# Two product-quantised layers of a vision block: where the tables' last rows are loaded and subtracted

## The chip, the cores and the metric

The kernel runs on one core of a Trainium2 chip. The core has five engines that run side by side, each with its own queue of instructions: TensorE (PE in the profile; its weight loads are PEld), VectorE (DVE), ScalarE (ACT), GpSimd (POOL) and SyncE (SP), which here only issues DMA transfers. The metric is the device time of one execution in microseconds (us); lower is better. Before the change three runs gave 3858.85 (median), 3858.28 and 3866.12.

## What is computed

The whole is a convolution block of three product-quantised layers (1024 to 256 channels, 3x3 on 256, 256 to 1024), and then an attention layer that the change does not touch. The first part, cut to what matters:

```python
def _amm(patches, centroids, lut, inv_temp):
    v = patches.reshape(B, ncb, sub, H * W).transpose(0, 3, 1, 2)
    scores = 2.0 * jnp.einsum('blcs,cks->blck', v, centroids) \
        - jnp.sum(centroids * centroids, -1)[None, None]
    attn = jax.nn.softmax(scores * inv_temp, axis=-1)      # over K = 16
    out = jnp.einsum('blck,cko->blo', attn, lut)

out = _amm(_gn(x), c1_centroids, c1_lut, c1_invt)          # layer 1
out = relu(_bn(out, bn1_g, bn1_b))
out = _amm(_extract3x3(out, 1), c2_centroids, c2_lut, c2_invt)  # layer 2
out = relu(_bn(out, bn2_g, bn2_b))
...
```

x is 32 images of 1024 x 14 x 14. A codebook has 16 entries, and its softmax weights over the 16 sum to one. So the sixteenth weight is one less the other fifteen: the table's sixteenth ("last") row can be subtracted from the other fifteen rows and need not have a weight of its own. This is what "last rows" means below.

## The kernel before

`layers()` builds the three layers in order; each engine runs its instructions in the order in which they are written, and waits by semaphores for what other engines and transfers must have finished. SP is one such queue: a transfer that must wait holds all transfers behind it. POOL's and DVE's orders are fixed in the same way.

**Units.** Layers 1 and 2 run 128 units each: 16 pairs of images times 8 groups b of codebooks. For one unit, `units()` writes score matmuls (PE), the exponential into a tile t (ACT, L595), a transpose (DVE, L607), in layer 1 a halving add (POOL, L610), the sum over 16 (DVE, L625), the reciprocal (L627), its transpose r (DVE, L633), the product t*r (POOL, L637), and then the table matmuls of PE (`lut`, L698): 16 of them, or 12 for b = 0 and 4. The scores run 4 units ahead of the table matmuls in layer 1, 3 in layer 2 (`ahead`), and t rotates over `ahead + 2` tiles. The order is written out by hand in the loop of `units()`: the scores of unit i + ahead, the softmax of an earlier one, its transfers, then `side(i)` (whatever else is due), then the table matmuls of unit i.

**Spare places.** 15 of 16 rows of t hold weights; the places of the sixteenth are used for more codebooks. Every fourth unit (b = 0 or 4) makes a "spare" block (L635), and `spare_rows` (L680) copies its rows into the free places of that unit's and the next three units' t, by 3 or 4 small transfers on SP. The table matmuls wait for these.

**Tables.** Each layer has 8 tables (`packed_lut`), in 8 weight tiles that layers 1 and 2 share: `own` loads the table's rows (L424), `others` the rows for the spare places (L427). `last_rows(d, layer, b)` loads the last rows, broadcast, to a place d: 3 or 4 transfers of 128 KB (L439) and, in its own `others`, one for the spare places (L442); `less` then subtracts d from the table (L445), on POOL. The table matmuls of unit b cannot start before that.

In layer 1, the first loads are x of pairs 0 and 1, tables 0 and 1 with their last rows, tables 2 to 7, and then one unit at a time the last rows of 2 to 7, in places of the unused output tile; the subtraction of b is at i = b - 3. In layer 2, the tables come in during layer 1's last units, as each weight tile comes free (`luts2`), and the last rows go through two places "drop" in turn: `without_last(b)`, at i = b - 2, subtracts the last rows of b and loads those of b + 2.

**Between the layers.** After layer 1's last table matmuls come the batch norm's constants (DVE, and one power on POOL, L242), its application into the pads (ACT, L917), their store to DRAM (`store_pair`, "h1d", L928), and from there the loads of 3x3 patches (`load_patches`, L948) that layer 2's score matmuls (L1001) read; L1010 adds the ninth tap. Meanwhile `score_biases` (L375 a copy on POOL, L377 and on for DVE, the matmul L390) and `score_matrices` (L351) make layer 2's score weights from its centroids, and `wm` (L982) those of the ninth tap. `warm` is a row of matmuls without a use of their result.

Of the kernel before, what the change touches and what calls it, by code (L numbers as in the profile page):

```python
# [10 lines left out]
F32 = mybir.dt.float32  # L11
AF = mybir.ActivationFunctionType
ALU = mybir.AluOpType
# [4 lines left out]
P = 128  # L18
C = 1024
CT = C // P  # L20
HW = 196
N2 = 2 * HW
NC = 448
NCP = 416
TP = 105
KC = 16
W = 256
IMG = 225
# [5 lines left out]
def bc(ap, axis, n):  # L34

    u = ap.unsqueeze(axis)
    shape = list(u.shape)
    shape[axis] = n
    return u.to_broadcast(shape)
# [111 lines left out]
def conv_preact_kernel(ctx: ExitStack, tc: tile.TileContext, a: dict, out: bass.AP):  # L151
    nc = tc.nc
    x = a["x"]
    B = x.shape[0]
    NP = B // 2
# [62 lines left out]
    def kmasks():  # L218
        nc.vector.tensor_reduce(kmask, ident.rearrange("p (c k) -> p k c", k=KC), AX.X, ALU.add)
# [24 lines left out]
    def load_x(pool, p):  # L244
        xt = pool.tile([P, CT, N2], F32, tag="x", name=f"x_{p}")
        for i in range(2):
            nc.sync.dma_start(
                xt[:, :, i * HW : (i + 1) * HW],
                x[2 * p + i].rearrange("(c q) n -> q c n", q=P),
            )  # L250
        return xt
# [107 lines left out]
    def score_biases(ps_tr, pool, tmp, i, raw, rows, groups, mask, per, order=None):  # L359

        n = groups * per
        room = tmp.tile([P, 4 * NCP], F32, tag="r", name=f"croom{i}")[:rows]  # L370
        sq = room[:, : groups * KC].rearrange("p (g k) -> p g k", k=KC)
        spread = room[:, 512 : 512 + P]
        cols = sq
        bias = pool.tile([P, n], F32, tag=f"cbias{i}", name=f"cbias{i}")
        nc.gpsimd.tensor_copy(spread.rearrange("p (c k) -> p c k", k=KC), bc(mask, 2, KC))  # L375

        nc.vector.tensor_tensor(sq, raw, raw, ALU.mult)  # L377
        centre(pool, i, "b", sq, -1.0)
        if per > 1:
            cols = room[:, 1024 : 1024 + n * KC].rearrange("p (g j k) -> p g j k", j=per, k=KC)  # L380
            nc.vector.tensor_tensor(
                cols,
                sq.unsqueeze(2).to_broadcast([rows, groups, per, KC]),
                mask4.unsqueeze(1).unsqueeze(3).to_broadcast([rows, groups, per, KC]),
                ALU.mult,
            )
            cols = cols.rearrange("p g j k -> p (g j) k")
        def biases():
            pb = ps_tr.tile([P, 512], F32, tag="tr", name=f"pb{i}")[:, : n * KC]
            nc.tensor.matmul(  # L390
                pb, spread, cols.rearrange("p n k -> p (n k)"), start=True, stop=True
            )
            pv = pb.rearrange("p (n k) -> p n k", k=KC)
            nc.vector.tensor_tensor(pv, pv, bc(kmask, 1, n), ALU.mult)
            b = pool.tile([P, n], F32, tag=f"cb{i}", name=f"cb{i}")
            nc.vector.tensor_reduce(b, pv, AX.X, ALU.add)
            dst, src = bias, b
            if order is not None:
                dst, src = order(bias), order(b, True)
            nc.vector.tensor_scalar(dst, src, -SHIFT, None, ALU.add)  # L400

        return bias, biases
# [28 lines left out]
    def last_rows(d, layer, b):  # L431


        rows, spare = unit_rows(layer, b), unit_rows(layer, b - b % 4)[0]
        j0 = 0 if b % 4 else 1
        v = weights[b].rearrange("p (s w) -> p s w", s=4)
        d = d.rearrange("p (s w) -> p s w", s=4)
        for j in range(j0, 4):
            nc.sync.dma_start(d[:, j], rows[j][:, 15:].to_broadcast([8, KC, W]))  # L439

        def others():
            nc.sync.dma_start(d[15::16, j0:], spare[:, 15:].to_broadcast([8, 4 - j0, W]))  # L442

        def less():
            nc.gpsimd.tensor_tensor(v[:, j0:], v[:, j0:], d[:, j0:], ALU.subtract)  # L445

        return others, less

# [77 lines left out]
    def layers(exact, early=None):  # L526
# [20 lines left out]
        pads = [  # L547
            big.tile([P, 2 * IMG], F32, tag=f"pad{k}", name=f"pad{k}") for k in range(2)
        ]
# [101 lines left out]
        def add_up(layer, n):  # L651
            if not exact:
                nc.vector.tensor_reduce(
                    sums[:, layer : layer + 1], added[:, :n].unsqueeze(1), AX.X, ALU.add
                )

        def unit_tiles(pool, ahead):

            ts = []
            for k in range(ahead + 2):  # L660
                t = pool.tile([P, 4, NCP], F32, tag=f"t{k}", name=f"t{k}")
                nc.gpsimd.memset(t[:, :, N2:], 1.0)
                ts.append(t)
            return ts
# [76 lines left out]
        with ExitStack() as s:  # L741
            once = s.enter_context(tc.tile_pool(name="p1c", bufs=1))
            xp = s.enter_context(tc.tile_pool(name="p1x", bufs=3))
# [3 lines left out]
            AHEAD = 2 if exact else 4  # L747
# [5 lines left out]
            def at(i, piece):  # L753
                todo.setdefault(max(i, -AHEAD - 1), []).append(piece)
# [47 lines left out]
            at(24, edges)  # L802
            at(40, masks2)
            for b in range(8):
                if b > 1:
                    at(b - 6, lambda b=b: load_last(b))
                    at(b - 5, lambda b=b: others(b))
                at(b - 3, lambda b=b: lasts[b][1]())

            def later():  # L810
                if not exact:
# [3 lines left out]
                load_raw2()  # L815

            at(16, later)
            for b in range(7):
                at(8 * (NP - 1) + b + 1, luts2[b][1])
                if b < 6:  # L820
                    at(8 * (NP - 1) + b + 2, luts2[b][2])

            for p in range(2):
                xts[p] = load_x(xp, p)
            luts = [packed_lut(1, b) for b in range(8)]

            lasts = []

            def load_last(b):
                d = out1[:, b // 4, NTOK - (b % 4 + 1) * C :][:, :C]  # L830
                lasts.append(last_rows(d, 1, b))

            def others(b):
                luts[b][2]()
                lasts[b][0]()

            for b in range(2):
                luts[b][1]()
                load_last(b)
            for b in range(2, 8):  # L840
                luts[b][1]()
            for b in range(2):
                others(b)
            if not exact:
                masks()
            bias1, biases = score_biases(ps_tr, once, st, 1, raw[1], P, CT, mask8, 4)
# [7 lines left out]
                f()  # L854
            if not exact:
                kmasks()
            biases()
            warm(14, xts[0][:, 1, :HW])
            gn[0][-1]()
# [6 lines left out]
            def score1(u):  # L866
# [8 lines left out]

            units(
                AHEAD,
                unit_tiles(once, AHEAD),
                st,
                [v for v, *_ in luts],  # L880
                score1,
# [5 lines left out]
                halve=not exact,  # L887
            )
            luts2[7][1]()
            add_up(0, 8 * NP)  # L890


        with ExitStack() as s:
            once = s.enter_context(tc.tile_pool(name="p2c", bufs=1))
            st = s.enter_context(tc.tile_pool(name="p2tt", bufs=1 if exact else 2))
            luts3 = []
            lasts = []

            def load_last(b):
                if b < 8:  # L900
                    t = st.tile([P, C], F32, tag="drop", name="drop", bufs=2)
                    lasts.append(last_rows(t, 2, b))

            def without_last(b):
                lasts[b][0]()
                lasts[b][1]()
                load_last(b + 2)

            for k in (2, 3):
                t = once.tile([P, 2 * IMG], F32, tag=f"pad{k}", name=f"pad{k}")  # L910
                nc.gpsimd.memset(t, 0.0)
                pads.append(t)


            def store_pair(p, h):
# [19 lines left out]
            SPAN = 2 * IMG - LEAD  # L935
            pbuf = [
                once.tile([P, 2, 4, 2 * IMG], F32, tag=f"patch{k}", name=f"patch{k}")
                for k in range(NPB)
            ]

            def load_patches(n, b0=0, m=4, js=range(4)):
                p, h = divmod(n, 2)
# [9 lines left out]
                            ),  # L952
                        )

            luts2[6][2]()
            store_pair(0, 0)
            load_patches(0, 0, 1)
            load_patches(0, 1, 3)
# [61 lines left out]

            def side2(i):

                p = {1: 1}.get(i + ahead, (i + ahead + 9) / 8)
                if p in range(1, NP):
                    for h in range(2):
                        store_pair(int(p), h)
                if i == -ahead:
                    luts2[7][2]()
                    for b in range(2):
                        load_last(b)  # L1030
                for b in range(8):
                    if i == max(b - 2, 1 - ahead):
                        without_last(b)
                if i == 60:
                    bias3, biases = score_biases(ps_tr, big, st, 3, raw[3], P, 2, mask8, 4)
                    parts[3] = score_matrices(big, 3, "", raw[3], mask8), bias3
                    biases()
                next_lut3(i - 8 * (NP - 1) - 1)

            def next_lut3(b):  # L1040
# [5 lines left out]
            stats2 = big.tile([P, 2, NP, 6], F32, tag="stats", name="stats2")  # L1046
            units(
                ahead,
                unit_tiles(once, ahead),
                st,  # L1050
                [v for v, *_ in luts2],
                score2,
# [5 lines left out]
            )  # L1058
            next_lut3(7)
            add_up(1, 8 * NP)  # L1060


        with ExitStack() as s:
# [876 lines left out]
```

## Time and profile before

| | |
|---|---|
| three runs | 3858.28, 3858.85, 3866.12 us |
| profiled execution, own time | 3854.55 us |
| its span (first to last instruction) | 3852.8 us |
| mean granted TensorE clock | 0.98 |
| layer 1's units (first to last table matmul) | 46 to 863 us |
| layer 2's first table matmul | 913.64 us |
| layer 2 ends | about 1925 us |

In the profile's rows, L12 is line 12 of the kernel before; "out<-in" are the program's tile names; the number after it is how often; in square brackets stands how long the engine had been idle before the instruction, and what released it ("<-DMA", "<-POOL lut L445"). "SPq" is SP issuing transfers: the duration is the time of issue, not of the transfer. The row of a stretch gives its ends, its length, then busy time and number of instructions for each engine, the granted TensorE clock (1.00 is full speed), the mean busy share of the DMA engines and their GB/s. Lines of helpers stand for all their callers: L439 and L445 are both layers', L698 layers 1 and 2.

### The profile page before, as it was taken

The page shows a single profiled execution, that of the slowest core. Times are in us where ns is not written, and L with a number is a line of the kernel's source. Part 1 is how long each engine was busy: PE and PEld are TensorE (multiplying, and loading weights), DVE is VectorE, ACT ScalarE, POOL GpSimd, SP SyncE. Part 2 cuts the span into 40 slices and gives each one's busy share as a digit, 9 for nine tenths or more (in the row PEclk, how much of TensorE's full clock was granted, in tenths as well). Part 3 has the DMA queues.
Part 4 walks back from the last instruction along what each step waited for, and adds up shares of the span by engine and source line. Part 5 has one row for each costly group of instructions (what it writes and reads, how often), then busy time and mean ns, then how long its engine had stood idle before and what let it go on. Part 6 is the DMA issues. An engine that isn't in the chain of part 4 may idle for free. (4 is left out here: it accounts for less than half of the span.)

```text
span 3852.8 us, 49359 instructions
## 1 busy us (share of the span) xinstructions
PE 3661.6 (95%) x16211; PEld 2043.1 (53%) x16211; DVE 2982.0 (77%) x4281; ACT 1699.0 (44%) x3851; POOL 2340.2 (61%) x1418
## 2 busy tenths in 40 slices
PE   7899999996899999999999999998999999999998
PEld 4455555553444544445544444444666666666665
DVE  7989999985688888888743333332699999999996
ACT  3455555541233333333222112220867666776674
POOL 6989999982544544455411111111688888888887
PEclk8999999997999999999999999999999999999999
DMA  4111111114344443444211101111323322223221
GB/s 143 44 43 42 38 30 40 42 40 121 86 94 93 82 91 77 93 93 88 73 39 47 39 19 39 38 39 39 115 64 90 90 83 84 86 80 95 78 80 43
DMA packets 243009, 263.80 MB, mean 68 GB/s; under 512 B 32784, under 2 KB 240496, under 8 KB 242744
## 3 DMA queue, kind: packets, MB, share of 16 engines
q1 hardware_dynamic: 242168, 260.41, 25.3%
q8 instruction: 130, 2.13, 0.2%
q14 instruction: 135, 1.11, 0.1%
q10 hardware_dynamic: 576, 0.15, 0.0%
HBM read 171.88 MB, written 76.56 MB: 64 GB/s over the span
## 5 line engine op out<-in xcount | busy, mean ns | idle before, releaser
L637 POOL TENSOR_TENSOR t<-t,r 128x1664 f32<-128x1664 f32 (+2 forms) x284 | 1007.1, 3546 | 981.8 <-DVE r L633 715.2
L698 PE MATMUL po<-t,lut 128*128 128x392 f32 x3840 | 1346.7, 504 | 64.2 <-POOL lut L445 33.4
L698 PEld LDWEIGHTS po<-t,lut 128*128 128x128 f32 x3840 | 717.3, 192 | 663.9 <-issue 143.7
L595 ACT ACTIVATE t<-sc,cbias 128x392 f32<-128x392 f32 (+1 forms) x1136 | 579.9, 593 | 989.4 <-issue 493.7
L1450 PE MATMUL mm<-y,lut 128*128 128x392 f32 x2048 | 714.4, 495 | 3.0 <-ACT vt L1515 1.1
L1116 PE MATMUL po<-t,lut 128*128 128x448 f32 x1792 | 683.1, 542 | 1.7 <-issue 1.7
L607 DVE STREAM_TRANSPOSE tt<-t 128x1664 f32<-128x1664 f32 (+1 forms) x284 | 542.0, 1908 | 166.4 <-ACT t L595 155.6
L633 DVE STREAM_TRANSPOSE r<-rc 128x1664 f32<-128x1664 f32 (+1 forms) x284 | 546.6, 1925 | 35.3 <-POOL t L637 15.1
L1672 DVE SCALAR_TENSOR_TENSOR pa<-y,lepe_w,pa 128x406 f32<-128x406 f32 x900 | 539.1, 639 | 4.9 <-PE pa L1654 2.2
L1116 PEld LDWEIGHTS po<-t,lut 128*128 128x128 f32 x1792 | 339.5, 191 | 342.2 <-issue 341.9
L1450 PEld LDWEIGHTS mm<-y,lut 128*128 128x128 f32 x2048 | 370.4, 188 | 251.1 <-issue 8.6
L1125 DVE BATCH_NORM_STATS2 stats<-o 128x6 f32<-128x448 f32 x112 | 68.9, 617 | 489.9 <-ACT o L1124 489.9
L625 DVE TENSOR_REDUCE sm<-tt 128x104 f32<-128x832 f32 (+2 forms) x284 | 423.4, 1491 | 13.0 <-POOL tt L610 7.4
L610 POOL TENSOR_TENSOR tt<-tt 128x832 f32<-128x832 f32 x128 | 247.7, 1935 | 17.7 <-DVE tt L607 17.7
L1124 ACT COPY o<-po 128x448 f32<-128x448 f32 x112 | 59.0, 528 | 427.5 <-PE po L1116 383.2
L627 DVE RECIPROCAL rc<-sm 128x104 f32<-128x104 f32 (+1 forms) x284 | 229.5, 808 | 9.8
L1001 PE MATMUL sc<-patch,cw 64*128 64x392 f32 x1024 | 217.4, 525 | 13.9 <-DMA patch<-h1d 11.8
L638 ACT ACTIVATE sm<-sm 128x104 f32<-128x104 f32 (+1 forms) x284 | 84.9, 299 | 233.4 <-DVE rc L627 231.5
L1001 PEld LDWEIGHTS sc<-patch,cw 64*128 64x128 f32 x1024 | 92.7, 188 | 128.4 <-issue 79.2
L1635 POOL TENSOR_TENSOR qr<-qr,zb 128x784 f32<-128x784 f32 x64 | 117.5, 1850 | 62.0 <-DMA zb<-zd 54.4
L1303 ACT ACTIVATE w<-x,tb,gn_a 128x196 f32<-128x196 f32 x248 | 128.3, 517 | 51.8 <-DVE x L1317 35.9
L1494 POOL TENSOR_TENSOR kr<-k,cosq 128x784 f32<-128x784 f32 x64 | 104.2, 1628 | 54.3 <-DVE k L1471 42.5
(182 smaller groups left out, 4057.3 us busy)
## 6 DMA issues: line engine op xcount, KB each, us to landing
patch<-h1d SPq DMA_DIRECT2D x248, 162.8 KB
x<-in_x_dram SPq DMA_DIRECT2D x32, 784.0 KB
o3d<-o SPq DMA_DIRECT2D x14, 1792.0 KB
x<-in_x_dram SPq DMA_DIRECT2D x64, 392.0 KB
out_dram<-x SPq DMA_DIRECT2D x64, 392.0 KB
o<-o3d SPq DMA_DIRECT2D x62, 392.0 KB
h1d<-pad SPq DMA_DIRECT2D x96, 225.0 KB
t<-spare SPq DMA_DIRECT2D x960, 12.2 KB
```

Source lines behind the costliest of these rows:

```text
L595: nc.scalar.activation(t[:, j, : sc.shape[1]], sc, AF.Identity if exact else AF.Exp, bias=bias[:, j : j + 1],)
L607: nc.vector.transpose(tt, tf)
L610: nc.gpsimd.tensor_tensor(tv[:, :, :8], tv[:, :, :8], tv[:, :, 8:], ALU.add)
L625: nc.vector.tensor_reduce(sm, tv, AX.X, ALU.add)
L627: nc.vector.reciprocal(rc, sm)
L633: nc.vector.transpose(r, bc(rc, 2, KC))
L637: nc.gpsimd.tensor_tensor(tf, tf, r, ALU.mult)
L698: nc.tensor.matmul(po[h], luts[b][:, j, h * P : (h + 1) * P], ts[u % len(ts)][:, j, :N2], start=(b == 0 and j == j0), stop=(b == 7 and j = ...
L1001: nc.tensor.matmul(sc, w8[r, 8 * h + 4 * (j // 2) + g], grid(pbuf[n % NPB][r, j // 2, g]), start=True, stop=False,)
L1116: nc.tensor.matmul(po, luts[g][:, m * P : (m + 1) * P], t3[h][:, g % 4, :], start=(g == 0), stop=(g == 7),)
L1450: nc.tensor.matmul(pv(), w[kt][:, m0 : m0 + P], ywin(p, first + kt), start=(kt == 0), stop=(kt == 3),)
L1672: nc.vector.scalar_tensor_tensor(acc, neighbours(p, c, offset(k)), lw[:, c, k : k + 1], acc, ALU.mult, ALU.add,)
```

## The change

- In layer 1's last units, layer 2's last rows are loaded whole to three places of the x pool that no further x needs: those of b = 3, 4, 5 at units 112 to 114, of b = 0, 1, 2 at 120 to 122, of b = 6 and 7 at 125 and 126; each table's `others` one unit later.
- All eight subtractions of layer 2 are on POOL between the layers, after layer 1's batch norm; the "others" of tables 6 and 7 are both loaded before them. `load_last`, `without_last` and the "drop" places of layer 2 go away.
- In layer 1, tables 0 to 5 are loaded each with its last rows at the start, x of pair 1 after the first two; 6 and 7 follow at i = 0 and 1. The subtractions of b = 0 and 1 are written ahead of the first unit, those of 3, 5, 7 are on DVE, of 2, 4, 6 on POOL.
- The t tiles are allocated once for both layers, six of them (layer 2 had five); their constant columns are set once.
- The copy in `score_biases` is DVE's. The pads' clearing in layer 2 comes after the subtractions; the pools of layer 2 are opened in another order, and the patch buffers created in reverse.

```diff
-        nc.gpsimd.tensor_copy(spread.rearrange("p (c k) -> p c k", k=KC), bc(mask, 2, KC))
+        nc.vector.tensor_copy(spread.rearrange("p (c k) -> p c k", k=KC), bc(mask, 2, KC))
...
-        def less():
-            nc.gpsimd.tensor_tensor(v[:, j0:], v[:, j0:], d[:, j0:], ALU.subtract)
+        def less(engine=nc.gpsimd):
+            engine.tensor_tensor(v[:, j0:], v[:, j0:], d[:, j0:], ALU.subtract)
...
             for b in range(8):
-                if b > 1:
-                    at(b - 6, lambda b=b: load_last(b))
+                if b > 5:
+                    at(b - 6, lambda b=b: load_rows(b))
+                if b > 3:
                     at(b - 5, lambda b=b: others(b))
-                at(b - 3, lambda b=b: lasts[b][1]())
+                engine = nc.vector if b in (3, 5, 7) else nc.gpsimd
+                at(b - 3 if b > 1 else -99, lambda b=b, engine=engine: lasts[b][1](engine))
...
+            lasts2, room = {}, {}
+
+            def load_last2(b, k, n):
+                def piece():
+                    if n == 0:
+                        room[k] = xp.tile([P, CT, N2], F32, tag="x", name=f"x_{NP + k}")
+                    d = room[k].rearrange("p c n -> p (c n)")[:, n * C : (n + 1) * C]
+                    lasts2[b] = last_rows(d, 2, b)
+
+                return piece
+
+            end = 8 * NP
+            for k, bs in ((0, (3, 4, 5)), (1, (0, 1, 2)), (2, (6, 7))):
+                for n, b in enumerate(bs):
+                    i = end - 8 * (2 - k) + n + (0 if k < 2 else -3)
+                    at(i, load_last2(b, k, n))
+                    at(i + 1, lambda b=b: lasts2[b][0]())
...
-            for p in range(2):
-                xts[p] = load_x(xp, p)
...
-            def load_last(b):
+            def load_rows(b):
+                luts[b][1]()
                 d = out1[:, b // 4, NTOK - (b % 4 + 1) * C :][:, :C]
                 lasts.append(last_rows(d, 1, b))
...
-            for b in range(2):
-                luts[b][1]()
-                load_last(b)
-            for b in range(2, 8):
-                luts[b][1]()
-            for b in range(2):
-                others(b)
+            xts[0] = load_x(xp, 0)
+            for b in range(6):
+                load_rows(b)
+                if b == 1:
+                    xts[1] = load_x(xp, 1)
+                if b % 2 == 0 and b:
+                    others(b - 2)
+                    others(b - 1)
...
             luts2[7][1]()
+            luts2[6][2]()
+            luts2[7][2]()
+            for b in range(8):
+                lasts2[b][1]()
             add_up(0, 8 * NP)
...
-            def without_last(b):
-                lasts[b][0]()
-                lasts[b][1]()
-                load_last(b + 2)
-
             for k in (2, 3):
-                t = once.tile([P, 2 * IMG], F32, tag=f"pad{k}", name=f"pad{k}")
-                nc.gpsimd.memset(t, 0.0)
-                pads.append(t)
+                pads.append(once.tile([P, 2 * IMG], F32, tag=f"pad{k}", name=f"pad{k}"))
...
                 once.tile([P, 2, 4, 2 * IMG], F32, tag=f"patch{k}", name=f"patch{k}")
-                for k in range(NPB)
-            ]
+                for k in (1, 0)
+            ][::-1]
...
-            luts2[6][2]()
             store_pair(0, 0)
...
+                if i == -ahead:
+                    for t in pads[2:]:
+                        nc.gpsimd.memset(t, 0.0)
...
-                if i == -ahead:
-                    luts2[7][2]()
-                    for b in range(2):
-                        load_last(b)
-                for b in range(8):
-                    if i == max(b - 2, 1 - ahead):
-                        without_last(b)
```

More of the change, by code (lines that the diff above doesn't have):

```diff
@@ L655, in add_up, with unit_tiles @@
                 )
-        def unit_tiles(pool, ahead):
+        two = ExitStack()
+        tsp = two.enter_context(tc.tile_pool(name="p12t", bufs=1))
+        def unit_tiles(n):
             ts = []
-            for k in range(ahead + 2):
-                t = pool.tile([P, 4, NCP], F32, tag=f"t{k}", name=f"t{k}")
+            for k in range(n):
+                t = tsp.tile([P, 4, NCP], F32, tag=f"t{k}", name=f"t{k}")
                 nc.gpsimd.memset(t[:, :, N2:], 1.0)
@@ L817, in layers @@
             at(16, later)
+            lasts2, room = {}, {}
[12 more added lines that the diff above has]
+                    at(i + 1, lambda b=b: lasts2[b][0]())
             for b in range(7):
-                at(8 * (NP - 1) + b + 1, luts2[b][1])
+                at(end - 7 + b, luts2[b][1])
                 if b < 6:
-                    at(8 * (NP - 1) + b + 2, luts2[b][2])
-            for p in range(2):
-                xts[p] = load_x(xp, p)
+                    at(end - 6 + b, luts2[b][2])
             luts = [packed_lut(1, b) for b in range(8)]
             lasts = []
-            def load_last(b):
+            def load_rows(b):
+                luts[b][1]()
                 d = out1[:, b // 4, NTOK - (b % 4 + 1) * C :][:, :C]
@@ L856, in layers @@
                 kmasks()
+            ts = unit_tiles(AHEAD + 2)
             biases()
@@ L877, in layers @@
                 AHEAD,
-                unit_tiles(once, AHEAD),
+                ts,
                 st,
@@ L889, in layers @@
             luts2[7][1]()
+            luts2[6][2]()
+            luts2[7][2]()
+            for b in range(8):
+                lasts2[b][1]()
             add_up(0, 8 * NP)
         with ExitStack() as s:
+            st = s.enter_context(tc.tile_pool(name="p2tt", bufs=1 if exact else 2))
             once = s.enter_context(tc.tile_pool(name="p2c", bufs=1))
-            st = s.enter_context(tc.tile_pool(name="p2tt", bufs=1 if exact else 2))
             luts3 = []
[L897 to L902, printed above, removed]
-            def without_last(b):
-                lasts[b][0]()
-                lasts[b][1]()
-                load_last(b + 2)
             for k in (2, 3):
-                t = once.tile([P, 2 * IMG], F32, tag=f"pad{k}", name=f"pad{k}")
-                nc.gpsimd.memset(t, 0.0)
-                pads.append(t)
+                pads.append(once.tile([P, 2 * IMG], F32, tag=f"pad{k}", name=f"pad{k}"))
             def store_pair(p, h):
@@ L1048, in layers @@
                 ahead,
-                unit_tiles(once, ahead),
+                ts,
                 st,
@@ L1060, in layers @@
             add_up(1, 8 * NP)
+        two.close()
         with ExitStack() as s:
```

## The prediction

> **What bounds the kernel now.** I read the shares first, then a table of stretches, then the instructions in order of time where a stretch falls short. The page's shares and its costliest groups:
>
> ```profile
> span 3852.8 us, 49359 instructions
> ...
> PE 3661.6 (95%) x16211; PEld 2043.1 (53%) x16211; DVE 2982.0 (77%) x4281; ACT 1699.0 (44%) x3851; POOL 2340.2 (61%) x1418
> ...
> L698 PE MATMUL po<-t,lut 128*128 128x392 f32 x3840 | 1346.7, 504 | 64.2 <-POOL lut L445 33.4
> ```
>
> TensorE is busy 95% of the span, so only its idle and slow-clocked stretches can be saved. Half of the 64.2 us that the lut matmuls waited stands against one line, the subtraction L445. The stretches (microseconds; busy time and count of PE, PEld, DVE, ACT, POOL; granted clock, DMA share, GB/s) show where:
>
> ```profile
> 40.00:80.00 40.00, 25.02 (x81) 12.35 (x74) 28.14 (x31) 11.56 (x30) 39.07 (x18) 0.74 0.36 106
> 80.00:120.00 40.00, 40.00 (x157) 20.94 (x155) 36.27 (x40) 21.95 (x56) 40.00 (x17) 1.00 0.16 48
> 860.00:900.00 40.00, 33.22 (x92) 14.91 (x91) 24.94 (x43) 10.15 (x22) 6.62 (x12) 0.74 0.60 155
> 900.00:950.00 50.00, 29.87 (x103) 13.87 (x102) 27.36 (x18) 9.35 (x25) 17.49 (x6) 0.80 0.44 104
> 950.00:1000.00 50.00, 29.23 (x93) 14.09 (x94) 23.76 (x15) 8.08 (x20) 20.74 (x9) 0.79 0.40 100
> 1100.00:1900.00 800.00, 794.42 (x3270) 397.30 (x3263) 700.26 (x461) 268.75 (x683) 393.26 (x132) 1.00 0.40 85
> ```
>
> Layer 2 is bound by PE once it runs (794 of 800). Its first 100 us are not: PE 59 of 100, clock 0.8. At layer 1's start POOL is the full engine (39.07 and 40.00 of 40). The order of time in layer 2's first units:
>
> ```profile
> 911.78 1.80 POOL L445 TENSOR_TENSOR lut<-lut,drop 128x768 f32<-128x768 f32 x1 [15.50 <-DMA drop<-in_lut_dram]
> 913.64 6.22 PE L698 MATMUL po<-t,lut 128*128 128x392 f32 x12 [11.99 <-POOL lut L445]
> 954.79 2.34 POOL L445 TENSOR_TENSOR lut<-lut,drop 128x1024 f32<-128x1024 f32 x1 [11.59 <-DMA drop<-in_lut_dram]
> 957.19 7.94 PE L698 MATMUL po<-t,lut 128*128 128x392 f32 x16 [9.69 <-POOL lut L445]
> 969.68 4.22 PE L698 MATMUL po<-t,lut 128*128 128x392 f32 x12 [2.17 <-POOL lut L445]
> ```
>
> Each lut block waits for a subtraction, which waits for its rows, which are loaded only when one of two places is free. Unit 0 starts at 913.64 and unit 8 at 1018.05: 104.4 us. At the steady pace (16 matmuls 5.53 + scores 2.32, 7.85 a unit; with 12 matmuls 6.54) eight units are 6 x 7.85 + 2 x 6.54 = 60.2. So 44.2 us are lost here.
>
> **Part 1, layer 2's last rows.** Eight subtractions leave the first units and stand in one row on POOL between the layers: six of 2.35 and two of 1.80 = 17.7 us. Before, POOL had nothing there:
>
> ```profile
> 864.65 0.56 POOL L242 TENSOR_TENSOR sc<-bve,mhalf 128x1 f32<-128x1 f32 x1 [2.07 <-DVE bve L325]
> ...
> 865.90 0.68 DVE L377 TENSOR_TENSOR croom<-craw 72x512 f32<-72x512 f32 x1
> ...
> 874.00 10.33 SPq L948 DMA_DIRECT2D patch<-h1d  x24
> ...
> 883.60 2.02 ACT L595 ACTIVATE t<-sc,cbias 128x392 f32<-128x392 f32 x4 [17.06 <-PE sc L1010]
> ...
> 892.49 1.01 POOL L635 TENSOR_TENSOR spare<-t,r 128x392 f32<-128x392 f32 x1 [24.99 <-DVE r L633]
> ```
>
> POOL's 25 us of idleness would hide them, but they are not free. In the built program the tiles of layer 2's set-up come to lie in the places that the rows used, so four things wait for the eighth subtraction: DVE's set-up chain (its head is the copy L375, now DVE's), PE's bias matmul L390, the first patch load on SP, and the memset of the pads. Behind the patch load on SP stand all patches, and behind the chain every score. The row runs from 865.3 to 865.3 + 17.7 + eight gaps of 0.05 = 883.4. Two ways lead on from there to unit 0's scores:
> - DVE: from 865.90 to the end of wm (874.36 + 1.29) is 9.75; plus the copy 0.3: ends at 893.5.
> - PE: L390 3.4 after the head (869.33 against 865.90), 887; ten warm-up matmuls took 3.45 warm, at half clock 6.5, so about 5; eight L1001 at 1.6 and eight L1010 at 0.9 (their durations from 900 on): about 895.3.
>
> The patches (0.42 each from 883.5; the first twelve out by 888.5) are not last. The head of unit 0 goes from 883.60 to 895.3: **+11.7**. From there as before: DVE's transpose 2.1 later, 4.7 to r, 1.9 for it, 1.0 + 2.8 for POOL's two products: 907.8 (before, 896.3). But the spare rows of t(0), issued only at 900.55 because seven loads of 5.19 stood ahead on SP, leave at once, and land about 2.5 later: the first lut block starts near **910.8** rather than 913.64. Then 60.2 for eight units, and 2 for the cold clock and a patch wait (925.17 and 980.10 had 3.80 and 4.69 of these, with 31 loads on the same queue): unit 8 at 973 rather than 1018. **Gain 45**; bounds 33 (both patch waits stay, a subtraction's rows come 4 late) and 50.
>
> A rule that speaks against this: the Trainium skill, "TensorE: Matmul & The Clock Gate", Part 1: PE falls back to half rate after an idle window of some 3.4 us, and needs a busy one as long to come back. PE will idle from about 874 to 887. The row of before, where PE was never idle for long (ten warm-ups in 3.45), would put unit 0's head at 893.7; by the rule the first 3.4 us of them run at half rate, some 5 in all, and it is 895.3. I take the rule, because the blocks after a wait agree with it (12 matmuls 6.22 at 913.64, 4.22 at 969.68). Were PE not to come back in the warm-ups, all 26 matmuls up to L1010 would double: 899. In return the restarts at 913.64, 928.51, 957.19, 983.44 and 999.25 (blocks of 6.2 to 7.9) become one.
>
> **Part 2, the loads in layer 1's tail.** 31 L439 and eight L442 leave SP's queue of layer 2 and enter that of units 112 to 127. At 0.62 (the seven in 5.19 were 0.74) they are 24 us of SP over 16 units of 6.4 (102 us), beside 2.55 a unit for the spare rows and 1.0 for luts: 5.1 a unit on average, 6.8 in the fullest. Four units are 0.4 over: **+1**, range 0 to 3. The lut places are loaded as before, only the others of 6 and 7 now both stand before the h1d store (4 us later, hidden by the subtractions).
>
> **Part 3, layer 1's start.** Of eight subtractions (17.7 us) POOL did all between 34.70 and 95.3, while full. Now two run before the first halving add, which came after idleness; three go to DVE; 2.35 + 1.80 + 2.35 = 6.5 stay. POOL's load to unit 7 falls by 11.2, DVE's rises by 3 x about 1.35 (twice a DVE product of 128x512, 0.69) = 4.
>
> ```profile
> 31.56 1.93 POOL L610 TENSOR_TENSOR tt<-tt 128x832 f32<-128x832 f32 x1 [8.99 <-DVE tt L607]
> ...
> 66.58 1.16 DVE L271 BATCH_NORM_STATS2 gst<-x 128x6 f32<-128x196 f32 x4 [8.53 <-DMA x<-in_x_dram]
> 69.65 0.50 PEld L698 LDWEIGHTS po<-t,lut 128*128 128x128 f32 x2 [10.52 <-issue]
> 69.68 7.95 PE L698 MATMUL po<-t,lut 128*128 128x392 f32 x16 [9.92 <-DMA t<-spare]
> ```
>
> The third pair's x stands ahead of unit 2's spare rows and holds both DVE and PE. Its issue waits for POOL too (the spare rows of unit 1 are ahead of it), and comes at about 51 instead of 56.73. Following unit by unit, r of unit 7 comes at 84.6 (91.18) and of unit 12 at 116 (125.44); from there DVE sets the pace (6.4 a unit) and keeps the lead. PE cannot use all: unit 2 starts near 64 (69.68). Gain **7**, bounds 2 and 10.
>
> A rule against it: "SBUF — State Buffer", "SBUF: two separate sides": a DVE instruction with two SBUF inputs and a POOL one shut each other out of a shared port for the whole instruction. No row of this trace has such a pair at length. By it the three DVE subtractions would hold POOL 3 x 1.35 = 4 more, and the gain is 3 to 4. I take most of the bare sum, since POOL has 11 less to do, and keep 3 inside the range.
>
> **Smaller edits at nothing.** The copies L375 on DVE are 0.3 each, the tile memsets (0.75 + 0.65) lie beside other work, and six t tiles instead of five in layer 2 let DVE run one unit further ahead, where PE is full anyway. The order of the attention stage's engines is not touched.
>
> **Sum** against the profiled span: 3852.8 - 45 + 1 - 7 = 3801.8; its own time 3854.55 becomes 3803.5. The runs' median is 4.3 above that execution: 3858.85 - 51 = **3808**.
>
> **Rivals.**
> - *The new wait eats more* (15%): the rows' loads or the cold PE put unit 0 five to eight later and both patch waits stay (8.5). For: everything of layer 2's head now hangs on one instruction. Against: eight units alone lost 44.2. Gain 25 to 30 in all: 3831.
> - *Layer 1's start gives nothing* (15%): x and the spare rows bind there, or DVE with 4 us more. For: the waits at 66.58 and 69.68 are DMA's. Against: POOL full for 80 us. 3858.85 - 44 = 3815.
> - *Patches bind layer 2's head anyway* (3%): then the change moves nothing, 3859; against: only 8.5 us of such waits.
> - *Slower* (3%): SP in layer 1's tail. Each load of 128 KB could hold the queue longer than its issue (four spare rows took 7.68 behind the x load, 1.9 each, and PE waited 9.92). At p us a load the tail takes 39p + 16 x 3.55 against 102; it loses the whole 51 from p = 2.5. At 1.9 it loses 29 and the change gains still. Against: L439 at 0.62 to 0.74 in this trace. 3872 at p = 2.8.
>
> **The numbers.** The forecast has 60% (3798 to 3818), 4% go to more than it (all 44.2 lost, the 10 at the start gone: 3796). The range 3797 to 3834 takes in the first two rivals. A measurement of this kernel tells 0.2% (7.7 us) from no change: faster 0.94, same 0.03, slower 0.03.
>
> **What would show it.** Right: eight L445 in a row on POOL after 865 (shifted), no lut block waiting for POOL after that, the first patch load and DVE's copy right at the end of the row, first exponential some 30 after the row's start, and eight units in 62. In layer 1, r of unit 7 at about 85. Wrong: gaps in the row that name the rows' DMA; patch waits over 5; spare rows late in units 112 to 127; the POOL products of units 2 to 7 longer than 3.72 beside DVE's subtractions.

## The result

The changed kernel takes 3832.9 us (median of four runs, 3831.8 to 3842.7) where the kernel before takes 3859.8: the ratio is 0.9933, 95% interval 0.9913 to 0.9953. The forecast was 3808. The sign is right and the time lies at the upper end of the range, but the gain is 27, about half of the 51 that were worked out. The profile of the changed kernel is of the slowest of its four runs (3842.7); the other three lie between 3831.8 and 3833.7.

The page of the changed kernel, the line of the span and that of the table matmuls (L702 is L698 of before; L684 is L680, L963 is L948, L1015 and L1024 are L1001 and L1010):

```profile
span 3840.9 us, 49292 instructions
...
L702 PE MATMUL po<-t,lut 128*128 128x392 f32 x3840 | 1343.5, 503 | 29.8 <-DMA t<-spare 25.8
```

The 33.4 us in which table matmuls waited for a subtraction are gone: most of what is left (25.8 of 29.8) is put down to the spare rows of t. The stretches of the changed kernel, columns as before:

```profile
40.00:80.00 40.00, 29.78 (x104) 15.15 (x104) 37.43 (x43) 16.73 (x43) 37.27 (x17) 0.81 0.46 133
80.00:120.00 40.00, 37.92 (x144) 19.81 (x144) 38.86 (x42) 20.10 (x50) 39.36 (x16) 0.96 0.18 53
...
800.00:860.00 60.00, 53.09 (x183) 27.88 (x184) 46.39 (x36) 22.43 (x59) 51.82 (x20) 0.94 0.21 62
860.00:900.00 40.00, 22.91 (x62) 12.17 (x61) 18.13 (x35) 2.40 (x4) 19.40 (x12) 0.79 0.46 134
900.00:950.00 50.00, 42.85 (x158) 20.07 (x158) 39.15 (x26) 15.03 (x37) 18.73 (x7) 0.83 0.62 132
950.00:1000.00 50.00, 50.00 (x204) 25.17 (x204) 43.99 (x29) 17.94 (x46) 25.87 (x8) 1.00 0.40 85
```

Layer 2's first units now keep PE busy: 93 of the 100 us from 900 on (59 before), the last 50 at full clock. But the tail of layer 1 (800 to 860) has PE busy 53 of 60. In the kernel before it was 59.8:

```profile
800.00:860.00 60.00, 59.77 (x217) 32.05 (x210) 47.54 (x37) 23.05 (x60) 52.83 (x21) 1.00 0.17 51
```

Marks taken from the order of time (us):

| | before | after | before, order A | after, order A |
|---|---|---|---|---|
| table matmuls of unit 19, layer 1 | 191.17 | 188.68 | 190.04 | 187.35 |
| layer 1's last table matmul ends | 862.6 | 871.2 | 862.3 | 865.7 |
| layer 2's unit 0 | 913.64 | 919.40 | 913.52 | 912.81 |
| its unit 8 | 1018.05 | 987.55 | 1018.40 | 980.87 |
| attention stage begins | 2697.3 | 2667.3 | 2698.0 | 2657.3 |
| span | 3852.8 | 3840.9 | 3856.9 | 3818.0 |

The last two columns are explained with the first experiments. At the start of the attention stage the changed kernel is 30 ahead in its profile, and then the attention stage, which the change does not touch, takes 1173.6 instead of 1155.5.

The head of layer 2, first the row of subtractions and what it releases, then PE:

```profile
873.72 17.36 POOL L445 TENSOR_TENSOR lut<-lut,x 128x768 f32<-128x768 f32 x8
...
891.10 10.81 SPq L963 DMA_DIRECT2D patch<-h1d  x24
891.11 0.57 DVE L375 COPY croom<-mask 72x128 f32<-72x128 f32 x1 [10.77 <-POOL lut L445]
```

```profile
901.71 0.94 PE L1024 MATMUL sc<-pad,wm 32*128 32x392 f32 x8
...
919.40 4.22 PE L702 MATMUL po<-t,lut 128*128 128x392 f32 x12
...
929.13 1.64 PE L1015 MATMUL sc<-patch,cw 64*128 64x392 f32 x2 [4.00 <-DMA patch<-h1d]
...
987.55 4.22 PE L702 MATMUL po<-t,lut 128*128 128x392 f32 x12
```

The row has no gaps and lasts 17.4; copy and patch load start in the same tenth of a microsecond as it ends, and unit 0's last score matmuls begin 10.6 later.

### The profile page after: what moved, and what is told of

The parts are those of the page before. It is cut to its first block, busy times and chain, and to the rows that moved or that the text cites. A ratio compares the mean times of both kernels' runs of the same rounds, so it can differ in the third digit from the quotient of the medians.

```text
span 3840.9 us, 49292 instructions
## 1 busy us (share of the span) xinstructions
PE 3655.9 (95%) x16211; PEld 2045.9 (53%) x16211; DVE 3008.7 (78%) x4287; ACT 1697.0 (44%) x3851; POOL 2334.6 (61%) x1407
## 5 line engine op out<-in xcount | busy, mean ns | idle before, releaser
L702 PE MATMUL po<-t,lut 128*128 128x392 f32 x3840 | 1343.5, 503 | 29.8 <-DMA t<-spare 25.8
L702 PEld LDWEIGHTS po<-t,lut 128*128 128x128 f32 x3840 | 715.3, 192 | 627.3 <-issue 132.7
L1128 PE MATMUL po<-t,lut 128*128 128x448 f32 x1792 | 683.2, 542 | 1.6 <-issue 1.6
L1015 PE MATMUL sc<-patch,cw 64*128 64x392 f32 x1024 | 210.2, 521 | 7.1 <-DMA patch<-h1d 5.0
L638 ACT ACTIVATE sm<-sm 128x104 f32<-128x104 f32 (+1 forms) x284 | 84.9, 299 | 234.7 <-DVE rc L627 232.8
L1015 PEld LDWEIGHTS sc<-patch,cw 64*128 64x128 f32 x1024 | 90.8, 186 | 116.9 <-issue 67.6
L1471 ACT ACTIVATE e<-mm,kbd 128x392 f32<-128x392 f32 x128 | 74.2, 580 | 168.1 <-PE mm L1462 165.0
```

The lines of the kernel that those rows point to most:

```text
L702: nc.tensor.matmul(po[h], luts[b][:, j, h * P : (h + 1) * P], ts[u % len(ts)][:, j, :N2], start=(b == 0 and j == j0), stop=(b == 7 and j = ...
L1015: nc.tensor.matmul(sc, w8[r, 8 * h + 4 * (j // 2) + g], grid(pbuf[n % NPB][r, j // 2, g]), start=True, stop=False,)
L1128: nc.tensor.matmul(po, luts[g][:, m * P : (m + 1) * P], t3[h][:, g % 4, :], start=(g == 0), stop=(g == 7),)
```

## The experiments

The times are medians, of four to six runs or more; the kernel before ran beside each group (3856.3 to 3858.7). Differences taken from the ratios to it instead of from the medians agree within 3. The runs of one kernel scatter: with order A (below) the changed kernel's five go from 3819.7 to 3828.1. A difference of less than about 5 between two medians is therefore no more than a hint unless the traces show it too. Of the single edits to that kernel below, only the one that leaves the tail's loads out has an interval clear of its own.

**The order of the attention stage.** The planner of that stage goes through a Python set of engines, so a build may write one of two orders. The profile of before has one (A: the norm's matmul `mm<-gst` follows the first `mm<-vt,kt`), the profile after has the other (B: `mm<-q,kmm` follows).

```diff
-        engines = {p[0] for p in self.pieces}
+        engines = sorted({p[0] for p in self.pieces}, key=str, reverse=True)   # A; without reverse: B
```

> The kernel before, with the planner of the attention stage going through its engines in one fixed order (A, the one that the profile of before has). Theory 'the order of the attention stage moves between builds and is worth some 18 us': own time and median about 3855, attention stage (from layer 3's last table matmuls to the end) 1155.5 as in the profile of before. Rival 'only noise between executions': 3859 with the same scatter.

> The changed kernel with the same fixed order A. Theory: the gain up to the attention stage is 30 (layer 1's start 0 to 2.5, its tail -8, between the layers and layer 2's head +39), and the attention stage takes what it took before: 3825. Rival 'the change itself slows the attention stage by 18': 3842 here too.

> The changed kernel with the other order (B, the one that its profile has). Theory: 3842, 18 above order A. Rival 'noise': the same as with A.

Measured: 3857.5 for the kernel before with A; 3824.3 for the changed one with A (ratio to before 0.9916, 0.9903 to 0.9929); 3836.2 with B (0.9943, 0.9931 to 0.9955). The changed kernel's attention stage takes 1160.7 with A and 1170.9 with B. So the order is worth 10 to 12 (18 had been expected), and hides part of the gain in the pair of profiles; with one order the change is worth 33. All further kernels have order A, and are compared with 3824.3. 18 of the forecast 51 are still missing.

**Layer 1's tail without the loads.** 26 of 30 row loads and 7 of 8 small ones are left out; one table's rows serve all eight subtractions, so the result is another one.

```diff
...
-                    d = room[k].rearrange("p c n -> p (c n)")[:, n * C : (n + 1) * C]
-                    lasts2[b] = last_rows(d, 2, b)
+                    if b == 3:
+                        room["d"] = room[k].rearrange("p c n -> p (c n)")[:, :C]
+                        lasts2[b] = last_rows(room["d"], 2, b)
+                    else:
+                        lasts2[b] = (lambda: None, last_rows(room["d"], 2, b, False)[1])
```

> The changed kernel, order A, with 27 of 31 row loads and 7 of 8 loads for the spare places left out of layer 1's tail (one table's rows are subtracted from all eight, so the result is another one). Theory 'SP's queue in the tail holds the spare rows of units 124 to 127': layer 1 ends 8 us earlier, 3816 to 3817. Rival 'the late end comes from the t tiles or POOL, not from the loads': 3825 as with order A.

Measured: 3812.7, 11.6 less. From unit 19 to layer 1's end it takes 671.5, as the kernel before does (671.5 and 672.2); with the loads it was 678.4 (order A) and 682.5 (the profile after). From layer 1's end to unit 0 it takes 48.2, no less than with the loads (47.1 and 48.2). So what the loads cost, they cost in the tail. SP's order of time in the changed kernel shows how:

```profile
838.52 2.33 SPq L684 DMA_DIRECT2D t<-spare  x3
843.01 0.66 SPq L442 DMA_DIRECT2D x<-in_lut_dram  x1
843.72 2.52 SPq L439 DMA_DIRECT2D x<-in_lut_dram  x4
...
846.28 0.60 SPq L427 DMA_DIRECT2D lut<-in_lut_dram  x1
846.98 0.38 SPq L424 DMA_DIRECT2D lut<-in_lut_dram  x1
847.46 2.62 SPq L684 DMA_DIRECT2D t<-spare  x4
...
853.29 9.00 PE L702 MATMUL po<-t,lut 128*128 128x392 f32 x21 [5.28 <-DMA t<-spare]
```

SP ends issuing one unit's rows of t at 840.9 and then does nothing until 843.0: the small load L442 writes over places that the row loads L439 of the unit before (issued up to 837.9) also write, and must wait for them to land. Then come four row loads and two table loads, and the next rows of t leave at 847.46, 4.3 after POOL's product of that t (843.13). In the kernel before they left at 843.58, right after the product (843.56). PE waits 5.28, and starts again at a reduced clock: 21 matmuls take 9.00, where 16 take 5.53 elsewhere.

What a small load waited for in SP's queue between 780 and 870, in the changed kernel's profile (total, times, longest):

```profile
SPq L442 <- DMA x<-in_lut_dram: 6.8, 4, 3.4
```

The kernel before has waits of the same kind in the same stretch:

```profile
SPq L427 <- DMA lut<-in_lut_dram: 9.2, 4, 3.4
```

There L427 writes into a table whose rows (L424) are still landing. The three long waits end at 860.27, 864.81 and 869.12, when the last rows of t had already been issued (by 855.8), so no table matmul was held. The hold could be read before the change was made.

**The same loads on ScalarE's queue.** All work is done.

```diff
...
-            nc.sync.dma_start(d[:, j], rows[j][:, 15:].to_broadcast([8, KC, W]))
+            queue.dma_start(d[:, j], rows[j][:, 15:].to_broadcast([8, KC, W]))
...
-                    lasts2[b] = last_rows(d, 2, b)
+                    lasts2[b] = last_rows(d, 2, b, nc.scalar)
```

> The changed kernel, order A, with layer 2's last rows issued in layer 1's tail by ScalarE's queue instead of SP's; all of the work is done. Theory 'it is SP's order that holds the spare rows': layer 1 ends 7 to 8 earlier and the h1d store with it, 3813 to 3816, as with the loads left out. Rival 'it is the transfers themselves, or the waits now hold the exponentials on ScalarE': 3824 or more.

Measured: 3820.8, 3.5 less (within the scatter), and unit 19 to the end of layer 1 takes 679.4: no shorter. The hold moved to ScalarE: its exponential at 839.98 came after 3.83 without work, of which ScalarE spent 836.56 to 839.88 issuing five of the loads. Moving the queue alone doesn't shorten the tail.

**The small loads later.** Six of the eight, three units after their rows instead of one; and then all eight after the last rows of t.

```diff
-                    at(i + 1, lambda b=b: lasts2[b][0]())
+                    at(min(i + 3, end - 1), lambda b=b: lasts2[b][0]())
```

In the second kernel the new line has `at(end - 1, ...)`.

> The changed kernel, order A, with six of the eight small loads for the spare places in layer 1's tail three units after their rows rather than one; all on SP. Theory 'each of them holds SP until its rows have landed (2 to 4 each), and the rows of t stand behind': layer 1 ends 3 to 5 earlier, 3820. Rival 'it is the transfers of 128 KB themselves': 3824.

> The changed kernel, order A, with all eight small loads of layer 1's tail after the last rows of t. Theory 'SP is still held in the tail when they come three units late': layer 1's end as with the loads left out, from unit 19 on 671 to 672 rather than 673.4, and 2 to 4 less than with three units late; but tables 6 and 7 come later. Rival 'what is left is issue and the transfers of the rows': no better than 3817.7.

Measured: 3817.7 (0.9899, 0.9884 to 0.9914), 6.6 less; unit 19 to the end 673.4. PE's waits between 780 and 870, with the change as it is (order A), and with the small loads three units late (total, times, longest):

```profile
PE po L702 <- DMA t<-spare: 5.3, 2, 3.8
```

```profile
PE po L702 <- DMA t<-spare: 2.2, 2, 1.4
```

Single traces scatter here too, but all point the same way. From unit 19 to layer 1's end it takes 678.4 to 683.2 in the seven traces, of all those here, in which the small loads follow on SP one unit after their rows. It takes 673.4, 674.8 and 674.4 in the three in which they come later, and 671.5 without the loads. So the wait for the landing is worth some 7 by these marks (6.6 by the medians), out of some 10 (11.6). With all eight small loads last the kernel takes 3820.3, and unit 19 to the end 674.4: the tail gets no shorter, and POOL's row of subtractions then waits 3.60 for them. What remains of the tail's cost, 3 by the marks and 5 by the medians, is therefore not this wait. That leaves the issue of the row loads and their transfers, which these runs do not separate.

**Layer 1's start.** Put back in the changed kernel (old order of loads, all subtractions on POOL at i = b - 3), and done alone in the kernel before.

```diff
             for b in range(8):
-                if b > 5:
+                if b > 1:
                     at(b - 6, lambda b=b: load_rows(b))
-                if b > 3:
                     at(b - 5, lambda b=b: others(b))
-                engine = nc.vector if b in (3, 5, 7) else nc.gpsimd
-                at(b - 3 if b > 1 else -99, lambda b=b, engine=engine: lasts[b][1](engine))
+                at(b - 3, lambda b=b: lasts[b][1]())
...
-            xts[0] = load_x(xp, 0)
-            for b in range(6):
+            for p in range(2):
+                xts[p] = load_x(xp, p)
+            for b in range(2):
+                luts[b][1]()
                 load_rows(b)
...
```

> The changed kernel, order A, with layer 1's start put back: the old order of the first loads, last rows 2 to 7 one unit at a time, all eight subtractions on POOL at i = b - 3. The prediction's worth of that part, 7: 3831. Theory from the profile after (two subtractions wait for their rows in front of the first halving add, and r of unit 7 comes no earlier): 3824 to 3827.

> The kernel before, order A, with only the change at layer 1's start (order of the first loads, subtractions 0 and 1 ahead, 3, 5 and 7 on DVE; the t tiles and the copy as before). If that part is worth what undoing it in the changed kernel cost (8.3): 3849. If it is worth what the traces of before and after differ by at unit 19 (2.5 to 2.7): 3855.

Measured: 3832.6, so the part is worth 8.3 there by the medians and 5.8 by the ratios (0.9931, 0.9917 to 0.9944, against 0.9916). Alone in the kernel before it gives 3854.5 (0.9989, 0.9981 to 0.9998), 3 to 4. The reading from the marks of unit 19 (2.5) is near the second; the forecast 7 lies between. The runs do not say more than 3 to 8.

**The two subtractions ahead of the first unit.** POOL at the start of the changed kernel:

```profile
32.55 4.10 POOL L445 TENSOR_TENSOR lut<-lut,out 128x768 f32<-128x768 f32 x2 [10.36 <-DMA out<-in_lut_dram]
36.60 3.79 POOL L610 TENSOR_TENSOR tt<-tt 128x832 f32<-128x832 f32 x2
```

They wait for their rows, and the first halving add, ready before 31.6, stands behind them until 36.60.

```diff
-                at(b - 3 if b > 1 else -99, lambda b=b, engine=engine: lasts[b][1](engine))
+                at(b - 3, lambda b=b, engine=engine: lasts[b][1](engine))
```

> The changed kernel, order A, with the subtractions of b = 0 and 1 at i = b - 3 again instead of ahead of the first unit; all else as changed. Theory 'their wait for the rows (10.36) put the first halving add from 31.6 to 36.6': r of unit 0 near 35.6 again, and 2 to 4 less in all, 3820 to 3822. Rival 'x and the spare rows bind the start': 3824.

Measured: 3820.7, 3.6 less, which is within the scatter. The marks show more: unit 19 comes at 184.66, and at 184.60 and 184.79 in the two combinations below that have the same edit. Without it, order A, it comes at 186.24 to 188.50. So the new wait is real and worth some 2 to 3 at unit 19. What of that reaches the end is open: in this trace layer 1 ends at 867.9, later than the 865.7 of order A.

**Between the layers.** The subtractions left out (this loop removed, so the result is another one), and on DVE instead of POOL.

```diff
             for b in range(8):
-                lasts2[b][1]()
+                lasts2[b][1](nc.vector)
```

> The changed kernel, order A, with the eight subtractions between the layers left out (layer 2 then counts the last rows wrongly). The prediction's price of the row, 11.7 (set-up chain and patches behind it): 3812. Theory 'SP comes out of layer 1's tail so late that the h1d store ends at 880 and the patches cannot be fetched before 883': 3 to 5 less, 3820.

> The changed kernel, order A, with layer 2's eight subtractions on DVE instead of POOL. The three on DVE in layer 1 ended 1.08 after POOL let go, so the row of eight is 8.1 rather than 17.4; but tables 6 and 7 land only near 880 behind SP, so the row can end at 882 to 883 instead of 885.6: 3821. Rival 'the row's length sets it, as predicted': 9 less, 3815.

Measured: 3816.6 without them, 7.7 less, between the two expectations; 3819.3 on DVE, 5.0 less. DVE's row:

```profile
870.26 6.37 DVE L445 TENSOR_TENSOR lut<-lut,x 128x768 f32<-128x768 f32 x6
...
878.87 2.54 DVE L445 TENSOR_TENSOR lut<-lut,x 128x1024 f32<-128x1024 f32 x2 [2.24 <-DMA lut<-in_lut_dram]
```

Eight take 8.9, half of POOL's 17.4, but the last two wait for the rows for the spare places of tables 6 and 7, which SP, late out of the tail, issued at 876.6 to 878.5. From layer 1's end to unit 8 the traces have 115.1 with the row on POOL (order A), 111.0 on DVE and 107.1 without it. Row and SP are two bounds close behind one another. Without the row the first patches, which need the h1d store (issued from 881.21 on), still leave at 885.54. That is 16.1 after layer 1's end, where it was 19.9 with the row (order A); so leaving the row out does not bring 11.7.

**Combinations.** One with ScalarE's queue for five tables' rows, three subtractions on POOL ahead of the batch norm and five on DVE; and one of just the three edits shown above that had each gained alone (small loads three units late, layer 2's subtractions on DVE, layer 1's first two at i = b - 3). The first, against the two late subtractions:

```diff
...
-                    lasts2[b] = last_rows(d, 2, b)
+                    lasts2[b] = last_rows(d, 2, b, nc.scalar if k else nc.sync)
...
-                    i = end - 8 * (2 - k) + n + (0 if k < 2 else -3)
+                    i = (end - 16 + 2 * n, end - 5, end - 3)[k]
                     at(i, load_last2(b, k, n))
-                    at(i + 1, lambda b=b: lasts2[b][0]())
+                    at((i + 4, end - 2, end - 1)[k], lambda b=b: lasts2[b][0]())
+            for b in range(3):
+                at(end - 1, lambda b=b: lasts2[b][1]())
...
-            for b in range(8):
-                lasts2[b][1]()
+            for b in range(3, 8):
+                lasts2[b][1](nc.vector)
```

> A combination, order A: subtractions of layer 1's b = 0 and 1 at i = b - 3; layer 2's rows of b = 3, 4, 5 every second unit from 112 with their small loads four units later, on SP; those of 0, 1, 2, 6, 7 on ScalarE's queue once the last exponentials are written; subtractions 0 to 2 on POOL before the batch norm, 3 to 7 on DVE after it. Sum of -7 (tail), -9 (between the layers), -3.6 (start): 3806. If the transfers or the new waits take it back, 3815 or more.

> The changed kernel, order A, with three edits at once: small loads three units late (-6.6 alone), layer 2's subtractions on DVE (-5.0 alone), subtractions of layer 1's b = 0 and 1 at i = b - 3 (-3.6 alone). If they are separate terms: 3824.3 - 15.2 = 3809. If SP is one bound behind two of them: 3813 or more.

Measured: 3811.8 for the first. Its tail fell behind again:

```profile
841.24 5.66 ACTq L439 DMA_DIRECT2D x<-in_lut_dram  x8
847.00 0.29 ACT L638 ACTIVATE sm<-sm 128x104 f32<-128x104 f32 x1 [12.73 <-DMA x<-in_lut_dram]
847.62 4.04 SPq L684 DMA_DIRECT2D t<-spare  x4
848.27 7.50 ACTq L439 DMA_DIRECT2D x<-in_lut_dram  x8
852.05 0.59 SPq L427 DMA_DIRECT2D lut<-in_lut_dram  x1
852.16 8.49 PE L702 MATMUL po<-t,lut 128*128 128x392 f32 x16 [5.30 <-DMA t<-spare]
```

ScalarE came to its next compute instruction (L638) only at 847.00, after issuing row loads, and the four rows of t left SP just after that. They took from 847.62 to 851.7 to issue (2.6 elsewhere), while the row loads of the other queue were under way; PE waited 5.30. The second gives **3808.6** (0.9879, 0.9863 to 0.9896): 15.7 below the changed kernel with the same order, and some 48 below the kernel before. The three terms add up to 15.2; with single terms as uncertain as these, so close a match may be luck. It is the best version of these.

## Why the prediction was right or wrong

- **Part 2, the tail: the step that failed.** The prediction held 39 issues of 0.62 (there are 38) against SP's free time and got +1, at most 3. Measured: 11.6 by the medians, 7 to 12 by the marks. It took each load for its issue only. The small load that writes into the landing place of the row loads waits for their landing, and SP's queue with it: some 7 of the cost. The rival "slower" had the right place, SP in layer 1's tail with the rows of t behind it, but laid the hold on the 128 KB loads, which stayed at 0.63 each. Those that held were the small ones behind them.
- **The attention stage's order: a term put at nothing.** The prediction has it as not touched. The change does not touch it, but the build can: the two profiles have different orders, and the order is worth 10 to 12.
- **Part 1, the head: right in its mechanism, 4 to 6 too good.** From layer 1's end to unit 0 the forecast was 48.2 (910.8 less 862.6) and the profile has 48.2, order A 47.1. The ten warm-up matmuls, weighed between 3.45 and 6.5 and set at about 5, took 4.62 soon after PE's idle 15.77. Eight units were to take 62; they took 68.1, with 4.00 of patch wait and blocks at reduced clock (7.11 at 932.32, for 5.53). From layer 1's end to unit 8: 155.4 before, 116.4 after, a gain of 39 (41 with order A), for 45. One of the two patch waits stayed, although the row loads were gone from the queue; it lay within the forecast's bounds, but not in its sum.
- **The row between the layers.** Its length (17.4 for 17.7) and its end as the start of chain and patches are as forecast. Of the four waits on the eighth subtraction three are seen; that of the bias matmul L390 cannot be, because it comes after DVE's chain. What was missed is that SP came late too, so that the h1d store was issued only by 885.9 in the profile, and that DVE's three small products after the batch norm stood still beside POOL's subtractions (below).
- **Part 3, the start: the size near the forecast (3 to 8 for 7), the working not, so the size is in part luck.** r of unit 7 was to come at 84.6 and of unit 12 at 116; they came at 92.02 (no earlier than the 91.18 of before) and 123.02. The wait of the two first subtractions for their rows was not counted. The rule of the shared port, weighed and set aside, was right: see below.
- **The sum.** -41, +11.6 and -3 to -8 make -32 to -37; the pair with one order has -33. With order B in the changed kernel 22 are left by the medians of those runs; the first pair has 27, and the 5 between are scatter. The smaller edits (six t tiles, the copy on DVE, the pads' clearing) were not run alone.
- **The rivals.** "The new wait eats more" forecast 3831, close to the result, but by luck: it put the loss into layer 2's head, and the larger part stands in front of it, in layer 1's tail.

## What to carry to other kernels

When loads move to an idle-looking stretch of an in-order queue, count besides their issue whether one writes where another is still landing: that one holds the queue until the other has landed (up to 3.4 us here), and everything urgent stands behind it. Such waits can be read in the profile before the change, where they may do no harm yet. Put such a pair some units apart. Where a planner's order can differ between builds, fix it before two versions are compared.

## What the hardware showed

Here two instructions with two inputs from SBUF, one on DVE and one on POOL, did not run together. The subtraction on DVE in layer 1 of the changed kernel:

```profile
52.40 2.35 POOL L445 TENSOR_TENSOR lut<-lut,out 128x1024 f32<-128x1024 f32 x1
53.99 1.84 DVE L445 TENSOR_TENSOR lut<-lut,out 128x1024 f32<-128x1024 f32 x1
54.71 2.92 POOL L610 TENSOR_TENSOR tt<-tt 128x832 f32<-128x832 f32 x1
```

DVE ends 1.08 after POOL's end at 54.75, and the next POOL add, 1.93 elsewhere, takes 2.92: it waits for DVE. With POOL idle, as in the run with all eight subtractions on DVE, six of them took 6.37, or 1.06 each. The prediction had this rule ("SBUF — State Buffer" of the Trainium skill, "SBUF: two separate sides") and no row for it; the trace agrees. Between the layers, products of 128x1 on DVE, 0.16 each before, each wait out one subtraction on POOL:

```profile
873.78 1.75 DVE L327 TENSOR_TENSOR sc<-sc,bn_g 128x1 f32<-128x1 f32 x1 [0.67 <-POOL sc L242]
875.57 2.28 DVE L328 TENSOR_TENSOR bi<-mv,sc 128x1 f32<-128x1 f32 x1
877.88 2.26 DVE L329 TENSOR_TENSOR bi<-bn_b,bi 128x1 f32<-128x1 f32 x1
```
